# A Mamba-2 mixer with a ternary FFN on one core: group norm sums in the middle of a step, a second buffer for one exit, other turns for FFN results, taps and transposes

## The chip, the core and the metric

The kernel runs on one core of a Trainium2 chip. The metric is the device time of one execution in microseconds (us), as the median of several executions. TensorE is called PE here, VectorE DVE, ScalarE ACT, GpSimd POOL and SyncE SP. DMA transfers are issued from SP's queue and from POOL's queue; each of these works in order.

## The reference

The input x has 4 sequences of 256 rows and 512 columns (1024 rows in all). The result is x + mixer(LN(x)) * silu(ffn(LN(x))). Cut to what matters:

```python
xn = layernorm(x)
# the mixer: 128 heads of 64 channels (8192 channels), 8 groups of 1024 channels, state 128
gate, xBC, dt = split(xn @ in_proj_w.T)
xBC = silu(causal_conv4(xBC) + conv_b)            # x, B and C
dt = softplus(dt + dt_bias); A = -exp(A_log)
y = chunked_scan(x * dt, A * dt, B, C) + D * x    # decay products and a recurrence
y = y * silu(gate)
y = y * rsqrt(mean(y * y over a group's 1024 channels) + eps) * norm_w
s = y @ out_proj_w.T
# the FFN: 1792 hidden units, weights -1, 0 or 1 with a scale for each row
f = (silu(xn @ gate_w.T) * (xn @ up_w.T)) @ down_w.T
out = x + s * silu(f)
```

## The kernel before, in words

Everything runs under a hand-written schedule: on each engine instructions run in the order in which the program issues them. So a change in the place of a line changes what stands ahead of it on its engine, and nothing reorders it. PSUM banks come from four pools: `ps_proj` (3 banks: pg, pu, px, pq, pz), `ps_t` (1 bank: transposes, and pv), `ps_o` (2 banks: output projection) and `ps_y` (2 banks).

**Part A (`front`, the first 317 us).** LayerNorm of the first four 128-row tiles, then the FFN in 28 steps: 2 halves h of the rows with 14 blocks f of hidden units each. A step does `project_exact` for the gate (wg into pg), the Silu into sg on ACT, `project_exact` for the up weights (wu), the product sg*pu on DVE, and for the block before it `down` (wd into four banks pf). sg is split into a high part hh (ACT) and a low part hl (DVE), so that the two exact products carry fp32. In between, three times in each step, the loop calls `next(pieces)`: after sg's Silu, after sg's product, and between hh and hl. `pieces` is a chain of generators, each `yield` of which ends a turn: `first_pieces` (LayerNorm of tiles 4–7, then sums of tiles of x in `combine_x` and of weights in `combine_w`), `dt_pieces` (the step sizes), and `bc_pieces` for each group (projection of B and C in px and pq, copies into cpad and xpad on ACT, four convolution taps on DVE, Silu, the scores pg, L452). `ffn_out` takes a finished tile of pf, multiplies it by the scale on DVE (L299), applies Silu on ACT (L300) and stores it.

**Part B (the rest).** 64 steps i, each for a tile of 128 channels (2 heads), and two trailing steps. A step projects x and the gate with a Strassen–Winograd scheme of seven products (`product`, L173) into px, pq and pz, which ACT copies into pz (L813), gT (L824) and xpad (L838, L870). DVE does convolution taps and decay scans, ACT the exponentials of the decays (`decay_exp`, L605) and the Silus; `meet` multiplies decays by scores; PE transposes (tp) and forms y (`y_products`, py); `y_gate` makes yg, which is stored to DRAM. The squares of yg are summed over the eight tiles of a group in sqacc, by DMAs from POOL's queue that add (`sqacc<-sq`). At the start of the first step of a group's output projection (i = 10, 18, …, 58) `norm_sums` sums sqacc over channels (16 matmuls of one column, pv, L673), ACT takes the square root (sd), DVE the reciprocal (rs).

From i = 10 on each step also does a part of the output projection of the group two steps behind (`project_out`; og is the group, on its turn 0 to 7). Two turns make one sequence: the even one four products (a11·b11, s1·tw1, s2·tw2, s4·b22), the odd one three. The s are sums on DVE (`left_sums`, `left_factors`), the tw sums of weights (`right_factors`). Results leave through `leave` (L765) on ACT, scaled by rs, into sa or sb, and at the end of the odd turn go to DRAM with adding DMAs on POOL's queue: 512 KB from sa, 256 KB and 128 KB from sb. The last group goes straight to the output behind the loop.

Of the kernel before, what the change touches and what calls it, by code (L numbers as in the profile page):

```python
# [81 lines left out]
def mixer_ffn(ctx: ExitStack, tc: tile.TileContext, x, in_w, conv_w, conv_b, dt_bias, a_log, d_col,  # L82
# [106 lines left out]
    def front(pre, one_of, fp, f2, hp, wq):  # L189
# [59 lines left out]

        def ln_tile(t):  # L250

            nc.vector.tensor_scalar(xts[t], xts[t], mv[:, t, 0:1], rstd[:, t:t + 1],
                                    ALU.subtract, ALU.mult)
            p, tag = ((ps_o, "o"), (ps_y, "y"))[t // 2] if t < 4 else (ps_t, "t")
            tp = p.tile([P, KT, P], F32, name="tp", tag=tag)
            for k in range(KT):
                nc.tensor.transpose(tp[:, k, :], xts[t][:, k * P:(k + 1) * P], ident)
            return tp
# [36 lines left out]
        def ffn_out(h, pfs, tiles=range(4)):  # L295
            for i in tiles:
                pf = pfs[i]
                o = pre.tile([P, HID], F32, name="xt")
                nc.vector.tensor_mul(o, pf, ds_bc)  # L299
                nc.scalar.activation(o, o, AF.Silu)  # L300
                t = h * len(pfs) + i
                nc.sync.dma_start(ffn[t * P:(t + 1) * P, :], o)

# [71 lines left out]
        def first_pieces():  # L375
            for t in range(4, NT):
                ln_stats(t)
                if t % 2:
                    yield
            ln_std(4, 4)  # L380
            nc.vector.reciprocal(rstd[:, 4:], rstd[:, 4:])
            yield
            for t in range(4, NT):
                keep(t, ln_tile(t))
                yield
            for n in range(4):
                combine_x(n)
                if n == 2:
                    held["a"] = combine_w(held.pop("w"))
                yield  # L390
# [15 lines left out]
        def bc_pieces(g):  # L406
# [25 lines left out]
            product(pq, s4, x22, False)  # L432
            nc.vector.tensor_add(cpad_h[1], cpad_h[1], by_batch(pq))
            last_tap(i_c, cT, cpad)
            yield
            conv_taps(i_c, cT, cpad, (0, 1))
            last_tap(i_b, bT, xpad)
            yield
# [3 lines left out]
            conv_silu(i_c, cT)  # L442
            conv_taps(i_b, bT, xpad, (1, 2))
            yield
            yield
            conv_silu(i_b, bT)
# [64 lines left out]
        for t in range(5):  # L511
            if t < 4:
                ln_stats(t)
                ln_std(t)
            if t:
                nc.vector.reciprocal(rstd[:, t - 1:t], rstd[:, t - 1:t])
                tps.append(ln_tile(t - 1))
                busy(4)
            if t > 1:
                split_tile(xh, xl, t - 2, tps[t - 2])  # L520
# [4 lines left out]
        for n, (h, f) in enumerate(steps):  # L525
            if n + 2 < len(steps):
                load_ffn(n + 2)
            pg = project_exact(ws[0], xh, xl)
            sg = fp.tile([P, HALF], F32, name="sg")
            nc.scalar.activation(sg, pg, AF.Silu, scale=gs[:, f:f + 1])  # L530
            next(pieces, None)
            pu, wd = project_exact(ws[1], xh, xl), ws[2]
            if f == FT - 1 and h == 0:
                xh, xl = split_x()
                for t in range(4, NT):
                    split_tile(xh, xl, t, xnT[:, :, t * P:(t + 1) * P])
            nc.vector.scalar_tensor_tensor(sg, pu, us[:, f:f + 1], sg, ALU.mult, ALU.mult)
            if n + 1 < len(steps):
                ws = cast_ffn(n + 1)
            next(pieces, None)  # L540
            if last:
                down(*last)
                if f == 0:
                    done = last[0]
                    ffn_out(h - 1, done, (0,))
            if f == 0:
                pfs = [p.tile([P, HID], F32, name="pf", tag=tag)
                       for p, tag in ((ps_o, "o"), (ps_o, "o"), (ps_y, "y"), (ps_y, "y"))]
            hh = fp.tile([P, HALF], F32R, name="hh")
            hl = fp.tile([P, HALF], F32R, name="hl")  # L550
            nc.scalar.copy(hh, sg)
            if f == 0 and h:
                ffn_out(h - 1, done, (1,))
            next(pieces, None)
            nc.vector.tensor_tensor(hl, sg, hh.bitcast(F32), ALU.subtract)
            if f == 0 and h:
                ffn_out(h - 1, done, (2, 3))
            last = pfs, f, hh, hl, wd
# [111 lines left out]
    def norm_sums(sqacc):  # L670
        pv = ps_t.tile([P, NT], F32, name="pv", tag="t")
        for t in range(NT):
            nc.tensor.matmul(pv[:, t:t + 1], sqacc[:, t * P:(t + 1) * P], one,  # L673
                             start=True, stop=True)
        sd = small.tile([P, NT], F32, name="sd2")
        nc.scalar.activation(sd, pv, AF.Sqrt, bias=eps, scale=1.0 / (DIN // G))
        return sd
# [73 lines left out]
    with tc.manual_schedule():  # L751
        nc.sync.dma_start(gm, scores[0])
        ms, offs = {0: load_rows(0)}, {0: load_off(0)}
        xTs, gTs, yps, wos, rights, toms = {}, {}, {}, {}, {}, {}
        sqacc = rs = ya = outs = left = nxt = ob = sa = sb = None
        for i in range(CT + 2):
# [5 lines left out]
            def leave(po, row, col, layer):  # L762
                to = (sa[:, row, col * HH:(col + 1) * HH] if layer == 0 else
                      sb[:, row + col, :])
                nc.scalar.mul(to, po, rs[:, 2 * ob + row:2 * ob + row + 1])  # L765

            def project_out(between):
                nonlocal sa, sb, outs
                if on % 2 == 0:
                    sa = osp.tile([P, NC, HID], F32, name="sa")  # L770
                    sb = osp.tile([P, 3, HH], F32, name="sb")
                    outs = out_first(left, rights[og], leave)
# [5 lines left out]
            def left_sums():  # L778
                nonlocal ob, ya, left
                if og >= 0 and on % 2 == 0:  # L780
                    ob, ya = on // 2, nxt
                    left, sums = left_factors(ya)
                    for make in sums:
                        make()

            if not here:
                left_sums()
                project_out(lambda: None)
# [7 lines left out]
            if here and i > 0:  # L796
                offs[i] = load_off(i)
            if og >= 0 and on == 0:
                sd = norm_sums(sqacc)

# [14 lines left out]
            if lead:  # L815
                conv_silu(i - 1, xTs[i - 1])
                if i > 1:
                    decay_exp(ms[i - 1][0])
            elif old:
                decay_exp(ms[i - 1][1])  # L820
            if here:
                product(pq, s1, t1, True)
                product(px, s2, t2, False)
                nc.scalar.copy(gT[:, HALF:], px)  # L824
                if lead and i > 1:
                    decay_exp(ms[i - 1][1])
# [9 lines left out]
            if here:  # L836
                product(px, s3, t3, False)
                nc.scalar.copy(xpad_h[1], by_batch(px))  # L838
            for k in range(PER_G):
                if wg >= 0 and wn == come(k) + 1:  # L840
# [11 lines left out]

            if here:
                left_sums()
            if wg >= 0 and wn == PER_G - 1:
                rights[wg], toms[wg] = right_factors(wos[wg])
# [3 lines left out]
            if old:  # L860
                vs = values_0(i - 1, xTs[i - 1])
            if og >= 0 and on == 0:
                rs = small.tile([P, NT], F32, name="rs2", bufs=2)
                nc.vector.reciprocal(rs, sd)
            for n, turn in ((wg, PER_G - 1), (og, 0), (og, 1)):
                if n >= 0 and on == turn:
                    toms[n].pop(0)()
# [9 lines left out]
            if here:  # L877
                nc.vector.tensor_add(gT[:, HALF:], gT[:, HALF:], pq)  # L878
            if old and og >= 0:
                vs.append(values_1(i - 1, xTs[i - 1]))  # L880
# [16 lines left out]
            if here:  # L897
# [12 lines left out]
                if i:  # L910
                    decay_scan(ms[i][1])
                else:
                    decay_exp(ms[i][0])
                    decay_exp(ms[i][1])
            if here and i >= LEAD:
                decay_exp(ms[i][0])
            if og >= 0 and on % 2:
# [3 lines left out]
                else:  # L921
                    nc.gpsimd.dma_start(rows_b, sa, accum_op=ALU.add)
                nc.gpsimd.dma_start(rows_b[:, 0, :], sb[:, 0:2].rearrange("p n c -> p (n c)"),
                                    accum_op=ALU.add)
                nc.gpsimd.dma_start(rows_b[:, 1, HH:], sb[:, 2], accum_op=ALU.add)
            elif og >= 0 and on < PER_G - 2:
# [18 lines left out]
        left, sums = left_factors(yas[0])  # L945
        for make in sums + toms[G - 1]:
            make()
# [79 lines left out]
```

## Time and profile before

| | us |
|---|---|
| median of 3 runs | 1814.58 (1812.96 to 1814.66) |
| profiled execution | 1817.91 |
| its span | 1815.9 |
| PE busy in it | 1751.6 (96%) |
| DVE busy | 1448.0 (80%) |
| ACT busy | 1076.4 (59%) |
| POOL busy | 196.8 (11%) |
| mean granted PE clock | 0.987 of full speed |

All times inside the program are those of the one profiled execution, whose span is 2.0 us shorter than its time and whose time is 3.3 us above the median of the runs. A label such as "PE px L173 <- ACT xpad L838" is read: PE, about to run the instruction of line 173 that writes px, waited for the instruction of ACT on line 838 that writes xpad. The granted clock is the share of TensorE's full speed that the chip allowed in a stretch.

### The profile page before, as it was taken

How to read it: one execution, taken by the hardware profiler on the slowest of the kernel's cores; microseconds unless marked ns; L12 is line 12 of the kernel's file. 1: busy time of each engine (PE TensorE's matmuls, PEld its weight loads, DVE VectorE, ACT ScalarE, POOL GpSimd, SP SyncE). 2: the span in 40 equal slices, each digit the busy share in tenths (PEclk: the TensorE clock that was granted, in tenths of full speed). 3: DMA queues.
4: the chain of work that ended last, by engine and by line, in shares of the span. 5: the costliest groups of instructions: out<-in, count | busy, mean ns of one | idle time of the engine just before them, and what ended most of it. 6: DMA issues, size and time to landing. Idle time of an engine off the chain costs nothing.

```text
span 1815.9 us, 22579 instructions
## 1 busy us (share of the span) xinstructions
PE 1751.6 (96%) x8494; PEld 1123.5 (62%) x8494; DVE 1448.0 (80%) x1740; ACT 1076.4 (59%) x1424; POOL 196.8 (11%) x235
## 2 busy tenths in 40 slices
PE   8999999999899999999999999999999999999969
PEld 6665666455466666666666666666666666666657
DVE  5757575799978888888888888888888888888836
ACT  3644333577666666666666666666666666666620
POOL 3221121000000000111011101110111011101110
PEclk9999999999999999999999999999999999999979
DMA  6254552667736665777577757775777676767663
GB/s 220 76 186 160 188 174 105 211 216 216 257 117 200 195 210 179 201 197 208 178 202 196 208 178 202 196 209 178 202 197 210 176 202 199 209 174 204 178 193 139
DMA packets 164491, 342.69 MB, mean 189 GB/s; under 512 B 15392, under 2 KB 55968, under 8 KB 164384
## 3 DMA queue, kind: packets, MB, share of 16 engines
q1 hardware_dynamic: 141872, 288.82, 46.0%
q0 software_dynamic: 22512, 52.44, 16.4%
q8 instruction: 67, 1.10, 0.2%
q14 instruction: 40, 0.33, 0.1%
HBM read 236.08 MB, written 76.28 MB: 172 GB/s over the span
## 4 chain that ended last, share of the span: by engine, by line
PE 90%; ACT 3%; DVE 3%; DMA 2%; issue 1%; SPq 0%; POOL 0%; DVEq 0%; ACTq 0%
PE px L173 28%; PE po L711 21%; PE pq L173 13%; PE py L655 9%; PE pz L173 7%; PE pp L283 5%; PE pf L291 2%; ACT xpad L838 2%; PE tp L614 2%; PE pg L452 1%; PE pv L673 1%; DMA sqacc<-sq 1%; DVE cT L181 1%; DMA acc<-sb 0%; PE pd L315 0%
## 5 line engine op out<-in xcount | busy, mean ns | idle before, releaser
L173 PE MATMUL px<-xc,w 128*128 128x512 f32 x576 | 279.2, 607 | 20.1 <-ACT xpad L838 15.8
L602 DVE TENSOR_TENSOR_SCAN m<-m,after 128x1024 f32<-128x1024 f32 x128 | 292.1, 2282 | 0.0
L181 DVE SCALAR_TENSOR_TENSOR xT<-xpad,cw,xT 128x1024 f32<-128x1024 f32 x192 | 246.2, 1282 | 4.6
L173 PEld LDWEIGHTS px<-xc,w 128*128 128x128 f32 x576 | 104.4, 190 | 137.8 <-issue 97.8
L711 PE MATMUL po<-wo,ya 128*128 128x256 f32 x768 | 178.4, 382 | 0.0
L608 DVE TENSOR_TENSOR m<-m,gm 128x1024 f32<-128x1024 f32 x128 | 154.8, 1210 | 25.9 <-ACT m L605 25.9
L655 PE MATMUL py<-m,v 128*64 128x128 f32 x2048 | 162.2, 278 | 3.9 <-DVE v L631 3.9
L711 PEld LDWEIGHTS po<-wo,ya 128*128 128x128 f32 x768 | 142.6, 192 | 17.6 <-issue 0.3
L894 POOL DMA_DIRECT2D sqacc<-sq x55 | 47.6, 865 | 965.5 <-ACT sq L850 965.5
L173 PE MATMUL px<-xnT,w 128*128 128x512 f32 x288 | 143.6, 621 | 0.0
L173 PE MATMUL px<-xc,s 128*128 128x512 f32 x288 | 137.2, 599 | 2.5 <-ACT pz L813 2.5
L173 PE MATMUL pq<-xnT,s 128*128 128x512 f32 x288 | 136.2, 595 | 1.1 <-DVE xpad L859 1.1
L173 PE MATMUL pq<-xc,s 128*128 128x512 f32 x288 | 136.4, 596 | 0.3 <-DVE gT L878 0.3
L605 ACT ACTIVATE m<-m 128x1024 f32<-128x1024 f32 x128 | 135.3, 1058 | 0.8
L173 PE MATMUL pz<-xnT,w 128*128 128x512 f32 x288 | 135.3, 592 | 0.0
L655 PEld LDWEIGHTS py<-m,v 128*64 128x64 f32 x2048 | 118.0, 138 | 26.2 <-issue 19.8
L711 PE MATMUL po<-tw,sy 128*128 128x256 f32 x512 | 117.0, 382 | 1.4 <-ACT sa L765 1.4
L859 DVE TENSOR_TENSOR xpad<-xpad,pq 128x512 f32<-128x512 f32 x64 | 43.8, 684 | 85.8 <-ACT xpad L838 85.6
L614 PEld LDWEIGHTS tp<-ident,xT 128*128 128x128 f32 x512 | 64.3, 142 | 71.1 <-issue 70.9
L765 ACT ACTIVATE sb<-po,rs 128x256 f32<-128x256 f32 x84 | 39.9, 475 | 114.5 <-PE po L711 106.0
L711 PEld LDWEIGHTS po<-tw,sy 128*128 128x128 f32 x512 | 98.1, 192 | 15.4 <-ACT sa L765 1.8
L662 DVE TENSOR_TENSOR yg<-py,gT 128x512 f32<-128x512 f32 x128 | 83.8, 678 | 22.7 <-PE py L655 22.7
(170 smaller groups left out, 3093.3 us busy)
## 6 DMA issues: line engine op xcount, KB each, us to landing
m<-rows SPq DMA_DIRECT2D x128, 512.0 KB, 6.3
w<-in_in_w SPq DMA_DIRECT2D x133, 256.0 KB, 6.8
mo<-rows SPq DMA_DIRECT2D x128, 256.0 KB, 7.2
gated<-yg SPq DMA_DIRECT2D x64, 512.0 KB, 8.3
ya<-gated SPq DMA_DIRECT2D x30, 1024.0 KB, 7.1
sqacc<-sq POOLq DMA_DIRECT2D x55, 512.0 KB, 5.4
wo<-in_out_w SPq DMA_DIRECT2D x64, 256.0 KB, 7.2
acc<-sa POOLq DMA_DIRECT2D x24, 512.0 KB, 6.0
```

What stands on the lines that cost most here:

```text
L173: nc.tensor.matmul(pp, a[:, k, :], b[:, k, :], start=start and k == 0, stop=k == KT // 2 - 1, skip_group_check=not start)
L181: nc.vector.scalar_tensor_tensor(xT, xpad[:, :, k:k + L], cw[:, i, k:k + 1], xT, ALU.mult, ALU.add)
L283: nc.tensor.matmul(pp, w[:, k * P:(k + 1) * P], part[:, k, :], start=(k == 0 and part is xh), stop=(k == KT - 1 and part is xl))
L602: nc.vector.tensor_tensor_scan(m, m, after, 0.0, ALU.add, ALU.mult)
L605: nc.scalar.activation(m, m, AF.Exp)
L608: nc.vector.tensor_mul(m, m, gm[:, 0:T])
L614: nc.tensor.transpose(tp[:, b, :], xT[:, b, c * P:(c + 1) * P], ident)
L655: nc.tensor.matmul(py[d, q * P:(q + 1) * P], v[:, b, h, :], m, start=False, stop=stop, skip_group_check=True)
L662: nc.vector.tensor_mul(yg[:, 2 * i:2 * i + 2, :], ps[i], by_batch(gT[:, i * HALF:(i + 1) * HALF]))
L711: nc.tensor.matmul(po, a[:, k, :], b[:, k, :], start=start and k == 0, stop=k == HG - 1, skip_group_check=not start)
L859: nc.vector.tensor_add(xpad_h[1], xpad_h[1], by_batch(pq))
L894: nc.gpsimd.dma_start(sqacc, sq, accum_op=ALU.add)
```

## The change

- `ln_tile` is split into `ln_norm` (DVE) and `ln_turn` (transposes on PE). In `first_pieces` the normalization of each of tiles 4–7 is issued a turn earlier and its transpose a turn later; the sequence is one turn longer.
- In `bc_pieces` the last taps of C and B are issued together a turn later, ahead of the other taps, and B's tap 2 a turn after its tap 1.
- The first half's FFN results leave later: tile 0 behind hl of the second half's first step, tiles 1 and 2 after sg's Silu of the next step, tile 3 before `down` of that step. The second half's results are stored from POOL's queue.
- The exponentials of step 0's decays are issued in step 1, as in the other early steps.
- `norm_sums` moves from the start of the step to behind the product of s3, and its bank from `ps_t` to `ps_o`; the reciprocal moves behind the second sum into gT.
- sb has two parts instead of three, and the third is a tile of its own, sc, in two buffers. The left sums of step 64 are made in step 63.
- The last group's right factors are made behind the loop, alternating with its left sums; so they no longer stand on DVE ahead of the addition of the last tile's square to sqacc.

```diff
-        def ln_tile(t):
+        def ln_norm(t):
             nc.vector.tensor_scalar(xts[t], xts[t], mv[:, t, 0:1], rstd[:, t:t + 1],
                                     ALU.subtract, ALU.mult)
+        def ln_turn(t):
...
-                nc.sync.dma_start(ffn[t * P:(t + 1) * P, :], o)
+                queue = nc.gpsimd if h else nc.sync
+                queue.dma_start(ffn[t * P:(t + 1) * P, :], o)
...
             nc.vector.reciprocal(rstd[:, 4:], rstd[:, 4:])
+            ln_norm(4)
             yield
             for t in range(4, NT):
-                keep(t, ln_tile(t))
+                if t + 1 < NT:
+                    ln_norm(t + 1)
                 yield
+                keep(t, ln_turn(t))
+            yield
...
+            yield
             last_tap(i_c, cT, cpad)
-            yield
+            last_tap(i_b, bT, xpad)
             conv_taps(i_c, cT, cpad, (0, 1))
-            last_tap(i_b, bT, xpad)
             yield
...
             conv_silu(i_c, cT)
-            conv_taps(i_b, bT, xpad, (1, 2))
+            conv_taps(i_b, bT, xpad, (1,))
             yield
+            conv_taps(i_b, bT, xpad, (2,))
             yield
...
             next(pieces, None)
+            if f == 1 and h:
+                ffn_out(h - 1, done, (1, 2))
             pu, wd = project_exact(ws[1], xh, xl), ws[2]
...
             next(pieces, None)
+            if f == 1 and h:
+                ffn_out(h - 1, done, (3,))
             if last:
                 down(*last)
                 if f == 0:
                     done = last[0]
-                    ffn_out(h - 1, done, (0,))
...
             nc.scalar.copy(hh, sg)
-            if f == 0 and h:
-                ffn_out(h - 1, done, (1,))
             next(pieces, None)
             nc.vector.tensor_tensor(hl, sg, hh.bitcast(F32), ALU.subtract)
             if f == 0 and h:
-                ffn_out(h - 1, done, (2, 3))
+                ffn_out(h - 1, done, (0,))
...
-        pv = ps_t.tile([P, NT], F32, name="pv", tag="t")
+        pv = ps_o.tile([P, NT], F32, name="pv", tag="o")
...
-                      sb[:, row + col, :])
+                      sc if row else sb[:, col, :])
...
-                    sb = osp.tile([P, 3, HH], F32, name="sb")
+                    sb = osp.tile([P, NC, HH], F32, name="sb")
+                    sc = osp.tile([P, HH], F32, name="sc", bufs=2)
...
+            if on % 2 == 0:
+                ob = on // 2
             if not here:
-                left_sums()
                 project_out(lambda: None)
...
-            if og >= 0 and on == 0:
-                sd = norm_sums(sqacc)
...
-                if i > 1:
-                    decay_exp(ms[i - 1][0])
+                decay_exp(ms[i - 1][0])
...
-                if lead and i > 1:
+                if lead:
                     decay_exp(ms[i - 1][1])
...
                 product(px, s3, t3, False)
                 nc.scalar.copy(xpad_h[1], by_batch(px))
+            if og >= 0 and on == 0:
+                sd = norm_sums(sqacc)
...
-            if here:
+            if og >= 0 and (here and on % 2 == 0 or i == CT - 1):
                 left_sums()
-            if wg >= 0 and wn == PER_G - 1:
+            if i < CT + 1 and wg >= 0 and wn == PER_G - 1:
...
-            if og >= 0 and on == 0:
-                rs = small.tile([P, NT], F32, name="rs2", bufs=2)
-                nc.vector.reciprocal(rs, sd)
...
                 nc.vector.tensor_add(gT[:, HALF:], gT[:, HALF:], pq)
+                if og >= 0 and on == 0:
+                    rs = small.tile([P, NT], F32, name="rs2", bufs=2)
+                    nc.vector.reciprocal(rs, sd)
...
-                else:
-                    decay_exp(ms[i][0])
-                    decay_exp(ms[i][1])
...
-                nc.gpsimd.dma_start(rows_b[:, 0, :], sb[:, 0:2].rearrange("p n c -> p (n c)"),
+                nc.gpsimd.dma_start(rows_b[:, 0, :], sb.rearrange("p n c -> p (n c)"),
                                     accum_op=ALU.add)
-                nc.gpsimd.dma_start(rows_b[:, 1, HH:], sb[:, 2], accum_op=ALU.add)
+                nc.gpsimd.dma_start(rows_b[:, 1, HH:], sc, accum_op=ALU.add)
...
-        for make in sums + toms[G - 1]:
+        rights[G - 1], toms = right_factors(wos[G - 1])
+        for make in (sums[0], toms[0], sums[1], toms[1], *sums[2:], *toms[2:]):
             make()
```

More of the change, by code (lines that the diff above doesn't have):

```diff
@@ L516, in front @@
                 nc.vector.reciprocal(rstd[:, t - 1:t], rstd[:, t - 1:t])
-                tps.append(ln_tile(t - 1))
+                ln_norm(t - 1)
+                tps.append(ln_turn(t - 1))
                 busy(4)
@@ L754, in mixer_ffn @@
         xTs, gTs, yps, wos, rights, toms = {}, {}, {}, {}, {}, {}
-        sqacc = rs = ya = outs = left = nxt = ob = sa = sb = None
+        sqacc = rs = ya = outs = left = nxt = ob = sa = sb = sc = None
         for i in range(CT + 2):
@@ L763, in leave @@
                 to = (sa[:, row, col * HH:(col + 1) * HH] if layer == 0 else
-                      sb[:, row + col, :])
+                      sc if row else sb[:, col, :])
                 nc.scalar.mul(to, po, rs[:, 2 * ob + row:2 * ob + row + 1])
             def project_out(between):
-                nonlocal sa, sb, outs
+                nonlocal sa, sb, sc, outs
                 if on % 2 == 0:
                     sa = osp.tile([P, NC, HID], F32, name="sa")
-                    sb = osp.tile([P, 3, HH], F32, name="sb")
+                    sb = osp.tile([P, NC, HH], F32, name="sb")
+                    sc = osp.tile([P, HH], F32, name="sc", bufs=2)
                     outs = out_first(left, rights[og], leave)
@@ L778, in left_sums @@
             def left_sums():
[L779 to L784, printed above, removed]
+                nonlocal ya, left
+                ya = nxt
+                left, sums = left_factors(ya)
+                for make in sums:
+                    make()
+            if on % 2 == 0:
+                ob = on // 2
             if not here:
-                left_sums()
                 project_out(lambda: None)
@@ L861, in mixer_ffn @@
                 vs = values_0(i - 1, xTs[i - 1])
-            if og >= 0 and on == 0:
-                rs = small.tile([P, NT], F32, name="rs2", bufs=2)
-                nc.vector.reciprocal(rs, sd)
             for n, turn in ((wg, PER_G - 1), (og, 0), (og, 1)):
-                if n >= 0 and on == turn:
+                if i < CT + 1 and n >= 0 and on == turn:
                     toms[n].pop(0)()
```

## The prediction

> **What bounds the kernel now.** First the page: which engine is full, and what the last chain is made of.
>
> ```profile
> PE   8999999999899999999999999999999999999969
> PEclk9999999999999999999999999999999999999979
> PE 90%; ACT 3%; DVE 3%; DMA 2%; issue 1%; SPq 0%; POOL 0%; DVEq 0%; ACTq 0%
> ```
>
> PE is 96% busy and 90% of the chain. The change removes no matmul, so it can save only PE's idle time and the time that PE runs at a lowered clock after being idle. Second, the list of PE's waits (wait, microseconds in all, times, longest):
>
> ```profile
> PE px L173 <- ACT xpad L838: 15.8, 64, 0.7
> PE po L711 <- ACT sb L765: 6.9, 1, 6.9
> PE tp L257 <- DVE xt L252: 6.8, 4, 3.3
> PE px L173 <- ACT cpad L417: 4.4, 1, 4.4
> PE tp L614 <- DVE v L622: 4.2, 1, 4.2
> PE pv L673 <- DMA sqacc<-sq: 3.9, 1, 3.9
> PE px L173 <- ACT pz L813: 2.5, 1, 2.5
> PE pg L452 <- ACT bT L186: 1.4, 1, 1.4
> ```
>
> Apart from the first row (0.24 us in each of 64 steps) these are single places, each beside an edit. Third, the table by stretches: PE, PEld, DVE, ACT, POOL busy, then granted clock, DMA share, GB/s.
>
> ```profile
> 150.00:200.00 50.00, 45.63 (x175) 30.25 (x174) 28.85 (x43) 16.84 (x26) 7.59 (x12) 0.93 0.41 145
> 490.00:523.00 33.00, 28.90 (x132) 19.04 (x132) 24.54 (x26) 19.21 (x24) 0.00 (x0) 0.84 0.33 116
> 523.00:1720.00 1197.00, 1184.32 (x6022) 749.46 (x6019) 1022.72 (x1191) 793.37 (x1054) 115.06 (x122) 1.00 0.68 196
> 1720.00:1760.00 40.00, 24.45 (x148) 20.14 (x143) 16.54 (x24) 11.29 (x16) 4.31 (x5) 0.82 0.63 173
> ```
>
> Two thirds of the span (523–1720) holds 12.7 us of idle PE at full clock: little to win there. The gains must come from the short stretches with a low clock. Fourth, PE's timeline there (start, duration, in brackets the idle time before):
>
> ```profile
> 179.52 3.78 PE L173 MATMUL px<-xc,w 128*128 128x512 f32 x4 [4.37 <-ACT cpad L417]
> 335.47 3.68 PE L173 MATMUL px<-xc,s 128*128 128x512 f32 x4 [2.47 <-ACT pz L813]
> 338.99 1.88 PE L173 MATMUL pz<-xnT,w 128*128 128x512 f32 x4
> 493.95 3.54 PE L673 MATMUL pv<-one,sqacc 128*128 128x1 f32 x16 [3.86 <-DMA sqacc<-sq]
> 497.35 3.76 PE L173 MATMUL px<-xnT,w 128*128 128x512 f32 x4
> 1726.02 1.99 PE L711 MATMUL po<-tw,sy 128*128 128x256 f32 x8 [1.38 <-ACT sa L765]
> 1734.95 3.67 PE L711 MATMUL po<-wo,sy 128*128 128x256 f32 x8 [6.93 <-ACT sb L765]
> ```
>
> The same four matmuls take 1.88 warm and 3.7 cold. So a wait is priced with what follows it: 2.47 us and more went cold here, 1.38 did not.
>
> **The change, part by part** (times of the profiled execution)
>
> 1. *LayerNorm tiles 4–7: each normalization a turn earlier, each transpose a turn later.* PE ended wg of step 1 at 18.8 and waited 3.33 for xt, whose normalization stood on DVE behind hl, which waited for hh; then 1.46 for the next tile. It took 11.2 us (18.8 to 30.04) for about 5.0 us of matmuls at warm durations, so 6.2 are lost. After, the first normalization stands directly after the reciprocal, and PE has wu's eight matmuls before the first transpose. Left: two waits of 0.2–0.3. Gain 5.7. combine_x and combine_w now come a turn later, behind u and sg's product on DVE (ended 50.47), so s2 is ready about 0.6 late: −0.6.
>
> 2. *FFN results of the first half.* Before, tile 0's Silu waited 5.01 on ACT for its DVE product (177.33), with cpad's copy queued behind it: PE waits 4.37, then runs cold, 7.3 lost. After, cpad's copy goes unhindered at about 174.6. But the new order on ACT is tile 0's Silu, sg, then xpad's copy; tile 0's product stands on DVE behind bT's tap, sums and hl and ends about 178.7. So xpad's copy moves to about 180.5, and px a22, which could start at 178.5, waits 2.05. This wait lies between 1.38 and 2.47, so its clock is open: gain 5.4 warm, 3.6 cold; I take 4.5. Tiles 1–3 leave later, with no matmul queued. The second half's four stores go from SP's queue to POOL's: POOL has no casts left, its nearest issue row is 865 ns, the results are read only near 1750, and SP's rows load waits for DVE (318.06) in either order: 0.
>
> 3. *Taps of the B/C pieces.* bT's last tap before the C taps, tap 2 a turn later. Before hl the taps remain, so pf's waits of 1.1 and 1.7 stay; pg's wait of 1.41 falls to about 0.7, and at the first piece bT's Silu may come 0.1–0.3 late. +0.5, bounds −1 and +1.5.
>
> 4. *The exponentials of step 0 move into step 1.* Gone: 1.28 table load and 2.00 of exp before pz's copy (wait 2.47, then cold: 4.3 lost). New: Silu of xT at its old place, then the load and the first exp (to 338.3) stand before gT's copy (338.9), and px s3 waits 336.2 to 338.95, 2.75. By the rows that goes cold (2.47 did), and a22 starts at 343.1 against 343.26; warm at 341.85. Bounds 0.2 and 1.4; I take 0.5, nearer the row.
>
> Here a rule speaks against the row. The Trainium skill (TensorE: Matmul & The Clock Gate, "HAM oscillation — how this bites in real kernels") says that the clock halves only after idle gaps above about 3.4 us. By it neither new wait (2.05, 2.75) goes cold and parts 2 and 4 give 6.8 together; by the row of 2.47, which did, as little as 3.8. I sum 5.0.
>
> 5. *Group sums of squares in the middle of the step.* At i=10 pv waited 3.86 for the accumulation sqacc<-sq (issued 482.33, landed 493.81), and pv, px and pq then ran cold. The step took 33.2 us (490.1–523.35), step i=18, with the same work, 25.06: 8.1 in excess. After, pv stands behind px s3, about 498.7, 5 us after that landing: gain 8.0. In all seven such steps the 0.24 wait for xpad's copy is now covered by pv's 2 us: 1.7. What is queued: sd's load and Sqrt wait for pv on ACT, behind them nw scaling and the square; by their durations the square ends 0.6 before the next px copy is due. rs moves behind gT's sum on DVE; its first reader, the leave, comes after px, pq and the first po. pv takes a bank of po's pool instead of tp's: the previous turn's leaves have read it. Seven table loads fewer (156 to 149) on ACT, 59% busy: 0.
>
> 6. *A second buffer for one exit, left sums of i=64 a step earlier.* At i=64 the leave into sb waited for both accumulations of the previous turn:
>
> ```profile
> ACT sb L765 <- DMA acc<-sb: 8.4, 1, 8.4
> acc<-sb POOLq DMA_DIRECT2D x1, 256.0 KB, 3.8
> acc<-sb POOLq DMA_DIRECT2D x1, 128.0 KB, 8.0
> ```
>
> Issued 1725.69 and 1726.27, they landed about 1729.5 and 1734.3. The chain from there: leaves, s4·b22 cold, last leave 1738.66, exp, meet, v, tp at 1743.28 (the 4.22 wait). After, the first of these leaves goes into the doubled sc, free since two turns; s4·b22 starts about 1727.75, and the last leave needs only the 256-KB transfer. It starts at max(1729.65, L), L between 1729.5 (its old landing) and 1734 (the ya loads now issue earlier, beside it; the median of this row over the run is 8.1). Gain 1738.66 minus that: 9.0 to 4.7. I take 6.5. The sa leave's 3.4 wait (1.38 on PE) stays.
>
> 7. *Tail: right factors among the left sums, the sqacc add first.* The add waited 3.59 for ACT's square anyway. rs comes about 2.4 later (1765.4), still before the first product of s1 ends (1766.35): 0.
>
> **Sum:** 5.7−0.6+4.5+0.5+0.5+8.0+1.7+6.5 = 26.8. The profiled execution (1817.91; span 1815.9, 2.0 around it) becomes 1791.1. It stands 3.3 above the median 1814.58, so the median becomes about 1788.
>
> **Rivals.**
> - *Forecast, chance 0.60:* gain 22–32, 1783–1793 in the median.
> - *Cooler, 0.21:* both new waits go cold (−1.8 of parts 2 and 4), sb's transfer lands at 1734 (−1.8), and more waits of this size appear on ACT in the front. Gain 14–22, about 1796. For it: the 2.47 row, and the crowded DMA at 1722–1740. Against: most gains come from waits that vanish.
> - *More, 0.12:* sb lands at 1729.5 (+2.5), both waits stay warm (+1.8), pv's cover helps each step's other waits: gain 32–38, about 1780.
> - *Slower, 0.04:* pv in the middle holds ACT in every group step: sd waits for pv, the square and px's copy behind it come late, and the next px product waits; its po bank would hold back project_out as well. It decides from (26.8+3.6)/7 = 4.3 us per group step. Against it: pv x16 takes about 1.97 warm, sd 0.27, a load 1.28, so about 3 in all against 2 of cover plus 0.6 slack. It would give 1819 or so.
> - *The change does not do what it says, 0.03:* the accumulation at i=10 lands later still and PE cools mid-step, the sb leave waits for another transfer: within 0.2%.
>
> **How the numbers follow.** 0.2% (3.6 us) is about what a measurement of this kernel can tell from no change. Likeliest 1788. The forecast and most of the two neighbours give 1778 to 1799. Faster by over 0.2%: 0.60+0.21+0.12 = 0.93; within: 0.03; slower: 0.04.
>
> **What would show it.** Right: the waits for sqacc<-sq, sb and cpad gone from PE's list, the xt row below 1; new rows px<-xpad L417 near 2 and px<-gT L824 near 2.7; granted clock of 490–523 from 0.84 to 1.00, and more than 0.82 in the stretch of the last steps; step i=10 near 25 us. Wrong: a new po wait of over 5 us for acc<-sb, px waits in every eighth step, or a cold x4 (3.7) behind each new wait.

## The result and the profile after

The changed kernel takes 1795.02 us in the median (1792.90 to 1795.49, 4 runs) against 1814.07 (4 runs) of the kernel before: a ratio of 0.9893, 95% interval 0.9876 to 0.9911. That is 19 us faster, where 26.6 were forecast (about 1788, range 1778 to 1799). The profiled execution takes 1795.49 with a span of 1793.0: 22.9 less span than the profile before.

The page of the changed kernel, in the lines that answer to those shown of before:

```profile
PE   9999999999899999999999999999999999999989
PEclk9999999999999999999999999999999999999989
PE 89%; DVE 6%; ACT 4%; issue 1%; DMA 1%; ACTq 0%; DVEq 0%; SPq 0%
```

PE is still nearly the whole chain. PE's waits (in all, times, longest; line numbers are the changed kernel's, so L846 was L838 before, L822 was L813, L832 was L824):

```profile
PE px L173 <- ACT xpad L846: 14.1, 57, 0.7
PE tp L624 <- DVE v L632: 4.2, 1, 4.2
...
PE px L173 <- ACT xpad L424: 2.9, 2, 1.6
...
PE tp L259 <- DVE xt L251: 2.5, 3, 0.9
PE px L173 <- ACT gT L832: 2.4, 1, 2.4
PE px L173 <- ACT pz L822: 2.2, 1, 2.2
PE px L173 <- ACT cpad L424: 2.0, 2, 1.1
PE pg L460 <- ACT bT L186: 1.3, 2, 0.8
```

The rows for sqacc<-sq (3.9), sb (6.9) and the single cpad wait of 4.4 are gone. New are xpad L424 and gT L832, which the prediction named, and pz L822 with the two small cpad waits, which it did not; the pz wait of before stood at another place, the end of step 0. The xt row was to fall below 1 and is 2.5, because 1.7 of it lie ahead of 13 us, before the parts that were changed. The stretches that had a low clock before, each moved along with its work (PE, PEld, DVE, ACT, POOL busy, then granted clock, DMA share, GB/s):

```profile
13.00:50.00 37.00, 35.19 (x138) 24.28 (x138) 20.36 (x34) 19.08 (x28) 10.96 (x16) 1.00 0.52 172
150.00:200.00 50.00, 48.40 (x197) 32.84 (x196) 34.71 (x50) 20.23 (x30) 7.42 (x11) 1.00 0.54 183
490.00:515.00 25.00, 24.65 (x129) 16.53 (x130) 20.74 (x23) 15.56 (x21) 0.00 (x0) 0.93 0.25 89
1700.00:1740.00 40.00, 31.64 (x204) 26.84 (x204) 20.87 (x26) 15.84 (x24) 5.04 (x5) 0.87 0.72 197
```

The front is warm (1.00 at both places, 0.95 and 0.93 before), the tail is better (0.87 after 0.82), but around i=10 the clock is only 0.93 (0.84 before), where 1.00 was forecast, and step i=10 takes 28.7 instead of the 25 forecast. PE's timeline says why:

```profile
486.26 1.88 PE L173 MATMUL pq<-xc,s 128*128 128x512 f32 x4
490.35 3.68 PE L173 MATMUL px<-xc,s 128*128 128x512 f32 x4 [2.22 <-ACT pz L822]
493.87 1.88 PE L173 MATMUL pz<-xnT,w 128*128 128x512 f32 x4
```

pv waits no more, but px now waits for pz's copy, and its four matmuls are cold. ACT's timeline at this place shows what holds the copy:

```profile
486.30 1.15 ACT L186 ACTIVATE xT<-xT,cb 128x1024 f32<-128x1024 f32 x1 [3.21 <-DVE xT L181]
487.46 1.28 ACT L615 ACT_TABLE_LOAD   x1
488.76 1.06 ACT L615 ACTIVATE m<-m 128x1024 f32<-128x1024 f32 x1
489.72 0.58 ACT L822 COPY pz<-px 128x512 f32<-128x512 f32 x1
```

From step 9 on, the Silu, a table load and the first exponential of a tile are issued in its own step, so ahead of the next step's pz copy. The Silu waits for the taps on DVE until 486.30. In step 9 no output projection yet fills PE meanwhile. The kernel before has the same order on ACT, with the same wait for the taps:

```profile
491.87 1.15 ACT L186 ACTIVATE xT<-xT,cb 128x1024 f32<-128x1024 f32 x1 [3.21 <-DVE xT L181]
493.04 1.28 ACT L605 ACT_TABLE_LOAD   x1
494.33 1.06 ACT L605 ACTIVATE m<-m 128x1024 f32<-128x1024 f32 x1
```

But there PE stood in pv's wait for the DMA until 493.95: the longer wait covered the shorter one.

The slow clock behind the wait of 2.22 is not there in every execution. In six of the kernels below the code and the wait at this place are the same (2.21 or 2.22). In three of them px's four matmuls stayed warm, and step i=10 took 1.6 to 1.7 less, as here with the last exponential moved:

```profile
489.58 1.98 PE L173 MATMUL px<-xc,s 128*128 128x512 f32 x4 [2.22 <-ACT pz L824]
```

In the other three the clock fell as it did in the changed kernel.

**Where the 22.9 us come from**, read from the start of the same matmuls in both traces (wg of each FFN step, pz's product of each step of part B):

| part | forecast | profile |
|---|---|---|
| 1 LayerNorm, net of the later weight sums | 5.1 | 4.1 |
| 2 FFN results at the half boundary | 4.5 | 5.3 |
| 3 turns of the taps | 0.5 | −3.8 |
| 4 exponentials of step 0 | 0.5 | 0.0 |
| 5 sums of squares: i=10, then 0.56 in each of 7 steps | 8.0 + 1.7 | 4.0 + 3.9 |
| 6, 7 tail | 6.5 | 9.4 |

### The profile page after: what moved, and what is told of

The parts are those of the page before. It is cut to its first block, busy times and chain, and to the rows that moved or that the text cites. A ratio compares the mean times of both kernels' runs of the same rounds, so it can differ in the third digit from the quotient of the medians.

```text
span 1793.0 us, 22592 instructions
## 1 busy us (share of the span) xinstructions
PE 1742.7 (97%) x8494; PEld 1117.4 (62%) x8494; DVE 1448.6 (81%) x1740; ACT 1066.0 (59%) x1417; POOL 197.3 (11%) x239
## 4 chain that ended last, share of the span: by engine, by line
PE 89%; DVE 6%; ACT 4%; issue 1%; DMA 1%; ACTq 0%; DVEq 0%; SPq 0%
PE px L173 27%; PE po L721 21%; PE pq L173 13%; PE py L665 9%; PE pz L173 7%; PE pp L285 4%; PE pf L293 2%; ACT xpad L846 2%; PE tp L624 2%; PE pg L460 1%; DVE cT L181 1%; PE pv L683 1%; DVE xT L181 1%; DVE bT L181 1%; DVE m L612 0%
## 5 line engine op out<-in xcount | busy, mean ns | idle before, releaser
L173 PEld LDWEIGHTS px<-xc,s 128*128 128x128 f32 x288 | 54.7, 192 | 73.0 <-issue 65.8
```

The costliest lines, as they stand in the source:

```text
L173: nc.tensor.matmul(pp, a[:, k, :], b[:, k, :], start=start and k == 0, stop=k == KT // 2 - 1, skip_group_check=not start)
```

## The experiments

Each is the changed kernel with one edit; the last two undo or change several places. "Ahead" is the difference from the changed kernel's trace at the same matmul; ratios are to the kernel before, with which the changed kernel has 0.9893 (0.9876 to 0.9911). The intervals of the smaller gains overlap this one, so these gains are read from the traces, of one execution each. Because of the clock, a gain of 1.7 at i=10, or at i=1 behind its wait of 2.44, is not credited to an edit by itself. Three kernels ran once only: the repeated product, the one tap edit and the last exponential.

**Group sums at their old place**

```diff
-        pv = ps_o.tile([P, NT], F32, name="pv", tag="o")
+        pv = ps_t.tile([P, NT], F32, name="pv", tag="t")
...
+            if og >= 0 and on == 0:
+                sd = norm_sums(sqacc)
...
                 nc.scalar.copy(xpad_h[1], by_batch(px))
-            if og >= 0 and on == 0:
-                sd = norm_sums(sqacc)
```

> The changed kernel with the group norm sums alone put back: at the start of the step, in the transposes' bank, reciprocal at its old place. Theory A (the accumulation's wait at i=10 was removed, but a copy's wait on ACT that it had hidden took half of its place; each of the seven group steps gained 0.56): 4.0 + 3.9 = 7.9 us slower than the changed kernel, profiled about 1803.4, with the wait pv<-sqacc<-sq of about 3.9 back. The forecast's own sum: 9.7 slower, 1805. Rival B (the gain at i=10 comes from the early part's shift against the DMA, not from the place of the sums): under 4 slower.

Ratio 0.9929 (0.9913 to 0.9945): about 6.5 us slower than the changed kernel. That is between the two expectations, nearer to A. The trace confirms the smaller term to the hundredth: in each of six group steps 1.79 are lost at pz's product and 1.23 are regained at the next one, a loss of 0.56. At i=10 the profiled execution (1796.35, the fastest of four; the others took 1800.08 to 1802.74) loses nothing:

```profile
485.96 2.11 PE L683 MATMUL pv<-one,sqacc 128*128 128x1 f32 x16 [1.63 <-DMA sqacc<-sq]
487.93 3.46 PE L173 MATMUL px<-xnT,w 128*128 128x512 f32 x4
```

The accumulation landed 9.2 us after its issue here, against 11.5 in the kernel before, so the wait was 1.63 instead of 3.86; the expected 3.9 did not come back in this execution. What the old place costs at i=10 depends on the landing. That the slower executions had a later landing is likely, but they have no trace.

**Ten early steps instead of nine**

```diff
-LEAD = 9
+LEAD = 10
```

> The changed kernel with the early form of a step (Silu and exponentials of the tile before behind pz's copy) kept up to tile 9 instead of tile 8, so that at i=10 pz's copy does not stand behind Silu, table load and exp on ACT. Theory A: the wait px<-pz of 2.22 and the 1.8 us that px's four matmuls run cold behind it go, 4.0 faster than the changed kernel, profiled about 1791.4; the granted clock of the stretch 490 to 515 goes from 0.93 to 1.00. Rival B (PE would wait at i=10 for DVE or the DMA anyway): under 1 us.

Ratio 0.9882 (0.9868 to 0.9897). The pz wait is gone, the four matmuls take 1.88 and the granted clock of 490–515 is 1.00. Up to pz's product i=10 gains 4.18, as A said, 2.5 of it the wait and what starts up behind it, the rest the clock. Then 1.69 go in the second half of the step, to a wait that was not there:

```profile
498.64 1.98 PE L173 MATMUL pq<-xnT,s 128*128 128x512 f32 x4 [1.42 <-DVE xpad L869]
```

The exponentials come later, so DVE's products behind them, then the left sums of the first output step, and xpad's sum behind those. Net 2.5: A for the place, but a wait for DVE, as in B, took back two fifths of the size.

**The taps at their old turns**

```diff
             nc.vector.tensor_add(cpad_h[1], cpad_h[1], by_batch(pq))
-            yield
             last_tap(i_c, cT, cpad)
-            last_tap(i_b, bT, xpad)
+            yield
             conv_taps(i_c, cT, cpad, (0, 1))
+            last_tap(i_b, bT, xpad)
...
-            conv_taps(i_b, bT, xpad, (1,))
-            yield
-            conv_taps(i_b, bT, xpad, (2,))
+            conv_taps(i_b, bT, xpad, (1, 2))
+            yield
```

> The changed kernel with the turns of the B and C taps alone put back. Theory A (a tap issued a turn later reads cpad or xpad longer, so the next copy into that buffer waits on ACT and PE behind it): the waits of 1.29, 0.47, 0.93 and 1.06 go and the pg wait of 1.41 is back, 3.8 faster than the changed kernel, profiled about 1791.6. Rival B (the waits come from the LayerNorm sequence's extra turn, which shifts every piece): under 1 us either way. The forecast said 0.5 slower.

Ratio 0.9873 (0.9856 to 0.9889), profiled 1789.90. At the last FFN step the kernel is 3.58 ahead (+1.54, −0.48, +0.84, +1.18, −0.13, +1.32, −0.57 and 0.1 lost before them). The waits for xpad (1.29), pg (0.47) and cpad (0.93 and 1.06) are gone and pg's 1.41 is back. So part 3 was a loss. The span is 5.1 shorter: 1.69 more came at i=1, where the wait of 2.44 is the same but the clock held. ACT's timeline of the changed kernel shows the mechanism:

```profile
84.24 0.59 ACT L424 COPY xpad<-px 128x512 f32<-128x512 f32 x1 [3.50 <-DVE bT L181]
...
140.24 0.59 ACT L424 COPY cpad<-px 128x512 f32<-128x512 f32 x1 [0.65 <-DVE cT L181]
```

The copies wait for DVE's taps, which still read the buffer that the next product is to be copied into. PE, which needs px again, waits behind the copy. (The cpad copy waited for DVE in the kernel before too, 0.80, but soon enough for PE.)

**One of the two taps' edits**: only the last taps at their old turns, B's tap 2 left late.

> The changed kernel with the last taps of C and B at their old turns, B's tap 2 left a turn late. Theory A (each buffer waits for its own late tap): the cpad waits of 0.93 and 1.06 go, the xpad wait of 1.29 at the first piece stays: 2.5 us faster than the changed kernel by the start of the last FFN step, where the old turns of all taps gave 3.6. Rival B (one cause for all): all waits go or none.

Between FFN steps 12 and 21 the two gains are 1.18 and 1.32, 2.5 together; the cpad waits are gone, and the xpad waits before 180 us stay at 2.6 in two. Each late tap holds its own buffer (A). At the start of the last FFN step the kernel is 2.8 ahead, where A said 2.5.

**The same product twice**

```diff
                 product(pq, s1, t1, True)
+                if i == PER_G + 2:
+                    product(pq, s1, t1, True)
```

> The changed kernel in which, at i=10 alone, the product s1*t1 into pq is computed twice (the second overwrites the first with the same values), so that PE has 1.7 us more work inside its 2.22 us wait for pz's copy. Theory A (half of the loss there is the lowered clock after the wait): the wait falls to about 0.5, px's four matmuls take 1.9 instead of 3.68, and with more work the kernel is 1.8 faster, profiled about 1793.7. Rival B (the four matmuls are slow for another reason, or a wait is all): no change, or up to 0.2 slower.

```profile
486.55 3.60 PE L173 MATMUL pq<-xc,s 128*128 128x512 f32 x8
490.65 1.98 PE L173 MATMUL px<-xc,s 128*128 128x512 f32 x4 [0.50 <-ACT pz L822]
```

The wait is 0.50, the four matmuls take 1.98, and step i=10 is 1.69 shorter with 1.7 us more work in it. So work inside the wait costs nothing, and the clock behind the wait is a cost of its own. That the work saved the clock is not shown: the three executions with the full wait and a warm x4 gained as much without it (1.64 to 1.70).

**Two exponentials later**

```diff
+                if i - 1 == LEAD:
+                    decay_exp(ms[i - 1][0])
                 decay_exp(ms[i - 1][1])
...
                 nc.scalar.copy(gT[:, HALF:], px)
+                if i == 1:
+                    decay_exp(ms[0][0])
```

> The changed kernel with two exponentials later on ACT: at i=10 the first of tile 9 (with its table load) behind pz's copy instead of ahead of it, at i=1 the first of tile 0 behind gT's copy. Theory A (ACT's order makes both waits): px<-pz 2.22 at i=10 and px<-gT 2.44 at i=1 fall to below 0.5 each, and no px x4 there takes over 2.0. 2.2 + 1.8 at i=10, and 2.4 at i=1 plus 0 to 1.8 for the clock: 6 to 8 us faster than the changed kernel, profiled 1787 to 1789. Rival B (the wait goes over to DVE, whose products of decays and scores are late, as xpad's sum was in the kernel with ten early steps, 1.4): 2 to 4.

Ratio 0.9877 (0.9857 to 0.9897); 4.2 ahead when part B ends. Both waits named are gone (less than 0.3 is left at each), so ACT's order did make them. But each has a follower. At i=10 4.07 are gained (the clock included) and 1.58 lost to xpad's sum, as with ten early steps. At i=1 the wait moves one copy on, because both exponentials and y's first copies now stand ahead of xpad's copy:

```profile
335.93 1.98 PE L173 MATMUL px<-xc,w 128*128 128x512 f32 x4 [2.60 <-ACT xpad L851]
```

The step up to i=2's mark takes 19.70, exactly what it takes in the kernel with old taps (19.72), which has the 2.44 wait but stays warm. The 1.7 gained against the changed kernel's trace are clock, not wait. B was right that the gain goes to the next wait, but at this place it is one for ACT, not for DVE.

**The exponentials of step 0 in step 0** (part 4 undone)

```diff
                 if i:
                     decay_scan(ms[i][1])
+                else:
+                    decay_exp(ms[i][0])
+                    decay_exp(ms[i][1])
```

> The changed kernel with the exponentials of step 0 in step 0 again. Theory A (one wait of 2.4 stands in the place of another, and which of them is followed by a low clock differs between executions): the wait px<-gT at i=1 goes, px<-pz of 2.5 at the end of step 0 is back, and the time is within 1.8 of the changed kernel's either way. Rival B (the forecast's step, counting both cold): 0.2 to 1.4 slower in every execution.

1794.05 us in the median, ratio 0.9879 (0.9863 to 0.9896). Step 0's mark loses 4.19 and step 1's gains 4.41, 0.2 together: part 4 trades one wait for another, as A said. Its trace ends 2.1 ahead of the changed kernel's all the same, 1.70 of it at i=10, where the code is the same but the matmuls behind the 2.21 wait stayed warm.

**One sb again**

```diff
-                      sc if row else sb[:, col, :])
+                      sb[:, row + col, :])
...
-                    sb = osp.tile([P, NC, HH], F32, name="sb")
-                    sc = osp.tile([P, HH], F32, name="sc", bufs=2)
+                    sb = osp.tile([P, 3, HH], F32, name="sb")
```

> The changed kernel with sb in three parts again and no sc, the left sums of step 64 still early. Theory A (the second buffer carries the gain in the tail): the wait po<-sb of about 6.9 is back, and the tail is about 9 us longer, profiled about 1804.5. Rival B (the early left sums carry it, by letting PE and the leaves start earlier): under 3 us longer.

Ratio 0.9930 (0.9914 to 0.9947). The tail is 7.5 longer (span 5.8 longer, though 1.73 ahead at the last mark of part B), with the wait back:

```profile
1710.66 1.99 PE L721 MATMUL po<-tw,sy 128*128 128x256 f32 x8 [1.24 <-ACT sa L775]
1719.01 3.78 PE L721 MATMUL po<-wo,sy 128*128 128x256 f32 x8 [6.35 <-ACT sb L775]
```

The second buffer carries the gain (A); the early left sums and part 7 can have at most the rest of the tail's 9.4.

**The last exponential ahead of the leaves**

```diff
+            if i == CT:
+                decay_exp(ms[i - 1][1])
             if not here:
                 project_out(lambda: None)
...
-            elif old:
+            elif old and here:
                 decay_exp(ms[i - 1][1])
```

> The changed kernel with the second exponential of the last tile ahead of step 64's leaves, in the 3.2 us in which ACT waits for acc<-sa. Theory A (the wait tp<-v of 4.2 comes from DVE's product of decays and scores, which waits 7.06 for that exponential behind the leaves): tp<-v falls to about 1, and up to 1.7 of cold py goes too: 3 to 5 us faster than the changed kernel, profiled about 1791. Rival B (the leave into sa starts late because of it, or y's first copies on ACT are next): under 1.5.

The tail is 5.05 shorter (7.5 in the span, less 2.46 that it was ahead before). In the changed kernel DVE waits 7.06 for this exponential, which stands behind the leaves on ACT while ACT waits 3.2 for a DMA:

```profile
1716.49 1.05 ACT L615 ACTIVATE m<-m 128x1024 f32<-128x1024 f32 x1
```

```profile
1717.57 1.23 DVE L618 TENSOR_TENSOR m<-m,gm 128x1024 f32<-128x1024 f32 x1 [7.06 <-ACT m L615]
```

Moved, PE's wait falls from 4.22 to 1.47 and the transposes behind it run at 0.63 instead of 1.09:

```profile
1715.33 0.63 PE L624 MATMUL tp<-ident,xT 128*128 128x128 f32 x4 [1.47 <-DVE v L632]
```

**LayerNorm and FFN results at their old places** (parts 1 and 2 undone, taps as changed: `ln_norm` again just ahead of its transpose, `ffn_out` again at f=0 around hh and hl, the second half's stores again from SP's queue)

> The changed kernel with LayerNorm of tiles 4 to 7 and the FFN results at their old places (parts 1 and 2 undone; taps as changed). Theory A: FFN steps 1 to 5 take 4.1 more (waits tp<-xt of 3.3 and 1.5 back), the step over the half boundary 5.3 more (wait px<-cpad of 4.4, and cold behind it): 9.4 slower, profiled about 1804.9. Rival B (with the taps' turns as changed the boundary has another order on ACT, so only part of the 5.3 depends on the results' places): 5 to 7 slower.

Ratio 0.9907 (0.9888 to 0.9926). LayerNorm's part is as read from the traces: −5.63, then +0.46 and +1.01, net 4.2. At the half boundary only 2.80 are lost, not 5.3: the cpad wait there is 3.06 and the four matmuls behind it take 2.74 (4.37 and 3.78 in the kernel before). With the old taps and the new results the same FFN step takes 16.47, with both old 21.62, with both new 16.34, with new taps and old results 19.14. So the two parts overlap here: either helps alone, and together they give little more than the results' places by themselves. In the two places together 7.0 are lost, the upper end of B; the span is only 5.3 longer, because at i=1 the clock held in this execution (1.70).

**All mends together**: old taps; tile 9's first exponential behind pz's copy, with the left sums (i=10) and the first weight sum (i=9) behind xpad's sum on DVE; at i=1 the second exponential, its product and y's first copies behind xpad's copy; the last exponential ahead of the leaves. Of this edit, the main lines that no experiment above has:

```diff
+            first = i in (PER_G + 1, PER_G + 2)
+            if first:
+                nc.vector.tensor_add(xpad_h[1], xpad_h[1], by_batch(pq))
+                vs = values_0(i - 1, xTs[i - 1])
             if og >= 0 and (here and on % 2 == 0 or i == CT - 1):
                 left_sums()
...
                 product(px, s3, t3, False)
                 nc.scalar.copy(xpad_h[1], by_batch(px))
+            if i == 1:
+                decay_exp(ms[0][1])
+                meet(ms[0][1], offs[0][1])
+                yps[0] = y_begin(0, xTs[0])
```

> The changed kernel with what the runs before point to, together: taps at their old turns (3.6), the exponential of tile 9 behind pz's copy at i=10 with the left sums there and the first weight sum at i=9 behind xpad's sum on DVE (4.1 and about 1 each, for the waits of 1.1 and 0.96), at i=1 the first exponential behind gT's copy and the second, with its product and y's first copies, behind xpad's copy (2 to 4), the last tile's second exponential ahead of step 64's leaves (5). Theory A (single waits in separate places add up): 14 to 18 us faster than the changed kernel, profiled 1778 to 1782. Rival B (each wait removed uncovers the next one, as at i=10): 8 to 12, profiled 1784 to 1788.

1780.98 us in the median (1779.54 to 1781.33), ratio 0.9807 (0.9791 to 0.9823): it beats both kernels. The span is 13.8 shorter and the median 14.0, at the lower end of A. The old taps give 3.2 by the end of the front, i=1 1.9, i=10 3.9 net, the tail 4.8; at i=1 and i=10 about 1.7 each is the clock, which the changed kernel's trace had lost at both. Missing is what i=1 was to give beyond the clock; the wait has moved again:

```profile
334.29 1.98 PE L173 MATMUL pq<-xnT,s 128*128 128x512 f32 x4 [1.74 <-DVE xpad L884]
```

## Why the prediction was right and where it failed

The direction held, the time is inside the range, and nearly all gains came at the places named. The likeliest case did not hold: 19.0 us lie below its 22 to 32. Of the difference between 26.6 and 19.0, about half is in the sum and half in its transfer to the median. That the sum missed by no more than 3.9 (26.8 for 22.9) is partly luck: part 3 and the term of i=10 were 8.3 too high, and the tail and the group steps, 5.1 too low, made up for much of it.

- *Part 1*: the first gain was as worked out, 5.57 for 5.7. The weight sums' give-back was 1.01, and 0.47 went at a transpose, against 0.6 in all.
- *Part 2*: the new xpad wait was 1.60 (2.05 forecast) and stayed warm, so the upper bound 5.4 was the right one (5.3). What the prediction did not see is that the changed taps alone would have taken part of it.
- *Part 3*: the step failed, and by more than its bounds (−1 to +1.5, measured −3.8). It followed who waits for a tap's result, pg and pf, and not who waits for the tap to have read its buffer. The next copy into cpad and xpad was never priced.
- *Part 4*: 0.0, just below its lower bound of 0.2. The 2.44 wait was forecast at 2.75.
- *Part 5*: the term of i=10 was mis-sized, 8.0 for 4.0. The excess of 8.1 was right, but the step "after, pv stands behind px s3: gain 8.0" assumed that nothing else was late there. A 2.22 wait lay under the 3.86 one. The kernels with ten early steps and with later exponentials show that wait and its cause. Of the missing 4.0, 2.2 are the wait and 1.8 the low clock behind it; in the executions in which the clock held there, the term is about 5.7. The cover in the group steps was worth 0.56 each instead of 0.24, which gave 2.2 back.
- *Part 6*: 9.4 with part 7, above the value taken and at the bound of 9.0 plus 0.4. The 256-KB transfer landed in 3.9, early enough that the last leave waited for PE alone; the bound L=1734 had no part.
- *The rule against the row.* The prediction weighed "a 2.47 wait goes cold" against the Trainium skill's threshold of about 3.4 us. Neither is a yes or no here. The table counts PE's waits in the thirteen traces of this case (both kernels and the eleven experiments, from 12 us on) and with how many a low clock came:

  | wait, us | times | low clock in it or just behind it |
  |---|---|---|
  | 0.9 to 1.5 | 73 | 0 |
  | 1.5 to 1.8 | 26 | 1 (the 1.63 ahead of pv) |
  | 2.2 to 2.6 | 19 | 12 |
  | 2.7 and more | 31 | 31 |

  The same wait of 2.44 at i=1 is followed by an x4 (four matmuls, 1.98 at full clock) of 3.68 in the changed kernel, 3.26 with ten early steps, 3.46 with the tail's exponential moved and 1.98 with old taps. In the clock records of these traces a low stretch lasts 3.41 us, or two or three times that, except where the program ends. One of 3.41 costs 1.7 where PE has work throughout, which is what i=10 and i=1 lost, and the x4 behind the wait catches all or part of it. The page's own remark (TensorE: Matmul & The Clock Gate, "What's actually happening") that the window is free-running and the count of slow matmuls at a kernel's start differs from run to run fits this; its threshold does not, since 12 of the 19 waits of 2.2 to 2.6 and all 16 of 2.77 to 3.33 were followed by a low clock.
- *From the profile to the median.* The profile before was 3.8 above its median, the profile after 0.5. The prediction took off the whole gain of one profiled execution. Over the executions of the kernel before, time goes with the mean clock: 1817.9 and 1818.1 at 0.987, 1816.5 to 1817.7 at 0.988, 1812.1 to 1816.0 at 0.989 to 0.990, 1810.0 and 1813.2 at 0.991. So part of what the profile before lost behind its waits was probably not lost in the median one. Which waits these were is open; only one execution of it has a trace.

Of the rivals, "Cooler" (14–22 us) has the right size and part of the causes. Of the two waits that it expected cold, gT's was and xpad's was not; small new waits on ACT did appear in the front, the buffers of the taps. But sb's transfer landed early, and the hidden wait at i=10 is in no rival. The slower rival did not occur: no group step has a new px wait.

## What to carry to other kernels

Before the removal of a wait is credited in full, ask which other wait ends inside it: find, for each engine that feeds the place, when its result would have been there without it. When an operation is issued later, price the release of what it reads as well as the arrival of what it writes. When the gains lie behind idle gaps of a few microseconds, count wait and slow clock apart and give the second a range: in these traces nothing below 1.5 us, anything from 0 to 1.7 at 2.2 to 2.6. A gain of that size between two single traces can be the clock alone; look for the same place in the traces of kernels that do not differ there. Before a whole gain is taken off the median, compare the clock of the profiled execution with that of the others.

## What was not expected of the hardware

The clock fell after waits of 2.2 us, and once after 1.63 (behind it 16 one-column matmuls, then an x4 of 3.46 instead of 1.98). The same wait in the same code gave 1.98 in one execution and 3.68 in another, and the low stretch was 3.41 us long or a multiple of it. One adding DMA of 512 KB, issued at the same point of the program, landed after 9.2 us in one execution and 11.5 in another.
